# Layer 1's constants made, and its first aggregate loaded, inside layer 0; another order of steps and slots in layer 1

## The chip, the cores and the metric

The kernel runs on one core of one Trainium2 chip. The metric is the device time of one execution in microseconds (us). The engines are named as in the profile: PE (TensorE, with PEld for its weight loads), DVE (VectorE), ACT (ScalarE), POOL (GpSimd) and SP (SyncE, which issues most DMAs).

## What is computed

There are 16 graphs of 1024 nodes with 256 features each (`x`), and a sparse 0/1 adjacency matrix `adj` for each graph. Two layers follow one another, in fp32:

```python
# layer 0, for graph b
Wh  = x @ W.T;  att = (Wh @ a1)[:, :, None] + (Wh @ a2)[:, None, :]
att = bn(leaky(bn(att)));  att = softmax(att, axis=2) * adj
x   = layernorm(x + elu(bn(att @ Wh)))        # bn: statistics over all graphs
# layer 1, for each of 4 heads
fts    = x @ W[h];  logits = f1[:, :, None] + f2[:, None, :]
coefs  = al * softmax(leaky(logits) - 1e9 * (1 - adj)) + (1 - al) * softmax(adj)
out[h] = elu(coefs @ fts + bias[h] + x)
x      = layernorm(x + mean(out))
```

The last `bn` of layer 0 takes its statistics over all graphs and nodes, so layer 1 can't begin with any graph before the last graph of layer 0 is aggregated.

## The kernel before

**Layer 0** has three stages. From 0 to 185 us PE transposes x (`px`, L279) and multiplies it by the weights (`pw`, L289), eight tiles per graph in two halves. ACT copies the transposes (`xT`, L285) and DVE copies each product out of PSUM (`wx`, L293; four PSUM buffers). x comes by SP's queue with six buffers (`load_x`, L226), each load issued behind the store of an earlier graph's `wx` (L294). After graph 1, `parameters1` (L190ff) loads layer 1's small parameters by SP: `bias1`, `fb_bc` and `al_bc`. From 185 to 310 us thresholds and sums for the batch norms are made, and from 310 to 797 us the 16 graphs are aggregated one after another, 30 us each (L572). Each graph's aggregate `hb` is stored to `h_dram` (L599).

**Between the layers**, DVE finishes the statistics (scale `s3` and shifts `t3` and `t31`; last line L1023), and then makes layer 1's constants in the pool `pk` (L1036 to L1134): `IW`, `MX`, `MY`, `bits`, `add`, `cols`, `far`, `rows`, `low`, `act`, `lanes`, `fws`, `xr`. One of them needs a load: `wl`, the last row of each head's weights, broadcast over the partitions (512 KB, L1120), is subtracted from `W1s` (L1122). `wl` has a buffer of the tag `rw` (two buffers), which the rows of the adjacency matrix use too. The tag `h` in `hpool` has one buffer.

**Layer 1** is written under a manual schedule: on each engine, instructions stand in the order of the program. For each graph there are 16 units (8 node tiles times 2 pairs of heads), and the loop at the end of the kernel goes over slots, one unit per slot. Unit n starts in slot n - 1 and ends in slot n + 11. Its steps, in order of their work:

- `gather` (L1550, PE): multiplies the gathered rows `xc` by the weights `w` into `pu` (three PSUM buffers); `invert` (L1608, DVE) takes the reciprocal `z`, and `norm` (L1616, ACT) makes `s`, `pu` scaled by `z`, in two or three instructions.
- `turn` and `turned` (L1622 PE, L1632 ACT) transpose `s` into `sT`; `linear` (L1642, PE) multiplies it by `W1s` into `pv`; `add` (L1650, DVE), `exps` (L1656, ACT) and `sum` (L1663 to L1671, DVE) make the elu and the mean over the heads.
- `mean`, `squares`, `span`, `power`, `close` and `store` (L1678 to L1712; DVE, ACT, DVE, POOL, ACT, SP) make the last layer norm and store it.

Beside the units of graph g, the side work for graph g + 1 is done: it is placed by the tables `AT`, `FETCH` and `WEIGH`, whose numbers are slots relative to that graph's first unit (a number of -28 is slot 4 of the graph two before, modulo 16). `side` sorts it into four lists, `early`, `first`, `after` and `late`, which `stand(0..3, n)` emits:

- neighbour lists: `load_rows` (L1147, SP, 1 MB each) brings half of the adjacency rows `rw`; `words` (L1156, PE) packs them into words `pc`; `worded` (L1167 ACT `fw`, L1171 DVE `wl`) copies them out; then come `places` and `placed` (`hi`, L1200), `low`, `high`, `pick` and `picked` (`po`, L1259, PE), `order`.
- the graph's input of layer 1: `exps` and `elu` of the aggregate `h` (L1418 and L1421 ACT, L1428 DVE; four pieces), `turn` (`pz`, L1434, PE), `residual` (L1444, DVE, with x loaded at L1403), `squares` (L1461, ACT, four at a time), `spans`, `factors`, `raised` (L1500 to L1503, ACT), `scale` (L1481, ACT, eight instructions, four to each half), `halve` (`xs`, L1516, DVE), `total` and `totalled` (`pX`, L1524 PE; `xr`, L1527 ACT), and the stores of the table `xe_dram` (L1508, L1509, L1530).
- the neighbours: `fetch` (L1338, POOL) gathers rows of that table by indirect DMA, five times for each of eight chunks and a few times for the shared groups `l`, `m`, `n` and `o`; `weigh` (L1353 to L1382 DVE, with one cast on ACT, L1360) makes their weights.

An engine takes its instructions in order, so an instruction that waits holds up all that stand behind it on the same engine. `turned(n, f, then)` puts a PE step into `first[n]` and the step that reads its result into `early[n + 1]`.

Of the kernel before, what the change touches and what calls it, by code (L numbers as in the profile page):

```python
# [27 lines left out]
def kernel(  # L28
# [170 lines left out]

    with ExitStack() as l0:  # L200
# [17 lines left out]
        with tc.tile_pool(name="apool", bufs=1) as apool, tc.tile_pool(  # L218
# [86 lines left out]
            mts = {b: mask(mpool, b, "mt0") for b in range(min(2, B))}  # L305

# [210 lines left out]
        with tc.tile_pool(name="wk", bufs=1) as wk, tc.tile_pool(  # L517
# [89 lines left out]
            for b in range(B):  # L607
                for n in range(NH * K):
# [6 lines left out]
                    if n == 1 and b + 2 < B:  # L615
                        mts[b + 2] = mask(mpool, b + 2, "mt0")
                    if n == 1 and b > 0:
                        store(b - 1, NH - 1)
# [406 lines left out]
    with ExitStack() as l1:  # L1025
        xpool = l1.enter_context(tc.tile_pool(name="x1pool", bufs=3))
        hpool = l1.enter_context(tc.tile_pool(name="hpool", bufs=1))
# [5 lines left out]


        TW = P + 2 * H
        IW = pk.tile([P, C, TW], F32, name="IW")  # L1036
        for oc in range(C):
            nc.vector.tensor_copy(IW[:, oc, 0:P], ident)
        nc.vector.tensor_copy(IW[:, :, P:TW], WW)

        QR = (H + 1) * QB
        MX = pk.tile([P, H, QB], F32, name="MX")
        MY = pk.tile([P, H, QB], F32, name="MY")
        nc.vector.tensor_tensor(
            MX, ident[:, 0 : H * QB].rearrange("p (h q) -> p h q", h=H),
            al_bc.unsqueeze(2).to_broadcast([P, H, QB]), ALU.mult,
        )
        nc.vector.tensor_tensor(  # L1050
            MY, ident[:, H * QB : QR].unsqueeze(1).to_broadcast([P, H, QB]),
            om_bc.unsqueeze(2).to_broadcast([P, H, QB]), ALU.mult,
        )
        nc.vector.tensor_tensor(MX, MX, MY, ALU.add)

        bits = pk.tile([P, QB], F32, name="bits")
        for i in range(QB):
            nc.vector.memset(bits[:, i : i + 1], float(1 << i))  # L1060
        ibits = pk.tile([P, QB], I32, name="ibits")
        nc.vector.tensor_copy(ibits, bits)
        nc.vector.memset(bits[:, QB - 1 : QB], -float(1 << (QB - 1)))

        every = pk.tile([P, 1], I32, name="every")
        nc.vector.memset(every, (1 << QB) - 1)

        add = pk.tile([P, K, NB + 1], F32, name="add")
        pick = pk.tile([P, NB, QB], F32, name="pick")
        nc.vector.tensor_tensor(  # L1070
            pick, ident[:, 0 : NB * QB].rearrange("p (n q) -> p n q", n=NB),
            bits.unsqueeze(1).to_broadcast([P, NB, QB]), ALU.mult,
        )
        nc.vector.tensor_reduce(add[:, 0, 0:NB], pick, AX.X, ALU.add)
        nc.vector.tensor_copy(
            add[:, 1:K, 0:NB], add[:, 0, 0:NB].unsqueeze(1).to_broadcast([P, K - 1, NB])
        )
        last = pk.tile([P, K, 3], F32, name="last")
        nc.vector.tensor_tensor(
            last, ident[:, NB * QB : P].unsqueeze(1).to_broadcast([P, K, 3]),  # L1080
            bits[:, 0 : 3 * K].rearrange("p (k q) -> p k q", q=3), ALU.mult,
        )
        nc.vector.tensor_reduce(add[:, :, NB], last, AX.X, ALU.add)
        add16 = pk.tile([P, K, NB + 1], BF16, name="add16")
        nc.vector.tensor_copy(add16, add)


        cols = pk.tile([P, K, NQ], FP16, name="cols")
        jj = pk.tile([P, K, NQ], I32, tag="pi", name="jj", bufs=1)
        nc.gpsimd.iota(jj, pattern=[[P, K], [0, NQ]], base=-N, channel_multiplier=1)  # L1090
        nc.vector.tensor_copy(cols, jj)
        in8 = pk.tile([P, 8], F32, name="in8")
        nc.vector.tensor_reduce(in8, ident.rearrange("p (r q) -> p q r", q=8), AX.X, ALU.add)
        in8h = pk.tile([P, 8], FP16, name="in8h")
        nc.vector.tensor_copy(in8h, in8)
        in16 = pk.tile([P, 16], F32, name="in16")
        nc.vector.tensor_reduce(in16, ident.rearrange("p (r q) -> p r q", q=8), AX.X, ALU.add)
        in16h = pk.tile([P, 16], FP16, name="in16h")
        nc.vector.tensor_copy(in16h, in16)
        far = pk.tile([P, 24], FP16, name="far")  # L1100
        for i in range(24):
            nc.vector.memset(far[:, i : i + 1], float(2048 + P + 16 * i))


        rows = pk.tile([P, 9, 8], F32, name="rows")
        nc.vector.memset(rows, float(N))
        nc.vector.memset(rows[0:1, 0:NB, :], float(N + 1))
        nc.vector.memset(rows[0:1, 6, 0:1], float(N + 1))

        low = pk.tile([P, K, 48], FP16, name="low")  # L1110
        nc.vector.memset(low, 99.0)
        act = pk.tile([P, K + 1, NQ], BF16, name="act")
        nc.vector.memset(act, 0.0)
        lanes = pk.tile([P, 16, 8], FP16, name="lanes")
        for i in range(16):
            nc.vector.memset(lanes[:, i], float(i))


        wl = pk.tile([P, H, F], F32, tag="rw", name="wl", bufs=2)
# [7 lines left out]
        for i in range(2):  # L1127
            nc.vector.memset(fws[i][:, :, 0:1], 1.0)
# [758 lines left out]
```

The softmax here doesn't subtract the row's maximum and nothing guards it: scores larger than these inputs give would overflow.

## Time and profile before

| | |
|---|---|
| median of 3 runs | 2366.42 us (2366.23 to 2368.56) |
| profiled execution | 2364.92 us |
| its span | 2363.2 us |
| mean granted clock of PE | 0.917 |

| stage (us of the span) | length | PE busy | DVE busy | ACT busy | DMA share |
|---|---|---|---|---|---|
| 0 to 185: x·W | 185 | 157.78 | 69.62 | 36.04 | 0.85 |
| 185 to 310: sums and thresholds | 125 | 48.34 | 90.71 | 68.90 | 1.01 |
| 310 to 797: aggregate | 487 | 477.81 | 446.27 | 345.02 | 0.66 |
| 797 to 812 | 15 | 0.66 | 9.97 | 1.52 | 0.52 |
| 812 to 865 | 53 | 26.15 | 26.42 | 22.84 | 0.42 |
| 865 to 900 | 35 | 17.83 | 25.32 | 5.40 | 0.59 |
| 992.14 to 1084.28: one graph of layer 1 | 92.14 | 87.81 | 80.19 | 61.30 | 0.66 |

Lines of the profile read so: in a wait list, "A x L1 <- B y L2: total, times, longest" says that engine A stood idle before its instruction for x at line L1, until B's instruction for y at L2 was done. In a timeline, a line gives the start, the duration, the engine, the source line, the operation, what it writes and reads, and in brackets the idle time before it with what ended it. The busy time of PE includes matmuls that are modelled from their issue; a busy PE is not PE at its peak.

### The profile page before, as it was taken

The numbers are of one execution on the slowest core, as the hardware profiler recorded it, in microseconds if no ns is written. First come the engines' busy times: TensorE is split into PE (matmuls) and PEld (weight loads), VectorE is DVE, ScalarE is ACT, GpSimd is POOL, SyncE is SP. The second block draws the span as 40 slices with busy tenths as digits, with TensorE's granted clock in tenths as the row PEclk, the third lists the DMA queues.
The fourth block names the chain that finished last, engine by engine and source line by source line (L and its number), as shares of the span: only waits on it lengthen the run. The fifth ranks groups of instructions, "written<-read, shape, count | busy, mean of one in ns | idle before, by whom it ended". The sixth has DMA issues, their size and how long they took to land. (4 is left out here: it accounts for less than half of the span.)

```text
span 2363.2 us, 36997 instructions
## 1 busy us (share of the span) xinstructions
PE 2105.5 (89%) x12503; PEld 1647.8 (70%) x12503; DVE 1916.6 (81%) x4800; ACT 1435.5 (61%) x3028; POOL 1060.5 (45%) x1133
## 2 busy tenths in 40 slices
PE   6992479999999549899999999999999999999997
PEld 5772434444444338788888888788888788887886
DVE  3334899999999357888988989888889789898886
ACT  1122777777777226567676675675676666756665
POOL 0000100000000036776767766767767667667682
PEclk9995589999999758899999999999999999999999
DMA  8969959985553348576675685675666756756651
GB/s 258 285 191 236 263 115 244 226 206 154 155 155 93 116 147 215 160 179 174 171 196 177 157 213 162 161 206 160 181 176 172 198 162 163 210 166 164 138 149 52
DMA packets 342359, 419.75 MB, mean 178 GB/s; under 512 B 172760, under 2 KB 273168, under 8 KB 336016
## 3 DMA queue, kind: packets, MB, share of 16 engines
q1 hardware_dynamic: 285840, 256.24, 36.7%
q0 software_dynamic: 55104, 158.54, 30.4%
q10 hardware_dynamic: 1216, 2.51, 0.3%
q8 instruction: 101, 1.65, 0.3%
q14 instruction: 98, 0.80, 0.1%
HBM read 346.47 MB, written 104.29 MB: 191 GB/s over the span
## 5 line engine op out<-in xcount | busy, mean ns | idle before, releaser
L1338 POOL DMA_INDIRECT xc<-xe_dram,ix x640 | 690.7, 1079 | 184.8 <-issue 166.3
L1642 PE MATMUL pv<-W1s,sT 128*128 128x256 f32 x2048 | 504.6, 390 | 0.3 <-ACT sT L1636 0.3
L572 PE MATMUL pa<-em,wh 128*128 128x512 f32 x1024 | 451.3, 599 | 17.8 <-DVE em L536 13.4
L1642 PEld LDWEIGHTS pv<-W1s,sT 128*128 128x128 f32 x2048 | 381.6, 197 | 44.0 <-ACT sT L1636 0.7
L1622 PEld LDWEIGHTS pt<-MX,s 125*128 125x128 f32 x2560 | 355.3, 206 | 31.0 <-ACT sT L1632 9.1
L572 PEld LDWEIGHTS pa<-em,wh 128*128 128x128 f32 x1024 | 193.9, 192 | 250.4 <-issue 237.3
L1550 PE MATMUL pu<-xc,w 128*125 128x256 f32 x1280 | 365.4, 401 | 0.0
L1622 PE MATMUL pt<-MX,s 125*128 125x100 f32 x2560 | 355.6, 289 | 4.8 <-ACT sT L1632 2.9
L1656 ACT ACTIVATE m<-v,neg 128x512 f32<-128x512 f32 x256 | 184.1, 719 | 251.0 <-DVE v L1650 199.6
L1616 ACT ACTIVATE s<-pu,z 125x256 f32<-125x256 f32 x640 | 260.6, 472 | 113.3 <-DVE z L1608 63.3
L1550 PEld LDWEIGHTS pu<-xc,w 128*125 128x125 f32 x1280 | 238.6, 197 | 37.5 <-issue 6.1
L528 ACT ACTIVATE e<-eb,c,s 128x1024 f32<-128x1024 f32 x128 | 155.0, 1236 | 79.0 <-DVE sm L542 42.6
L1632 ACT COPY sT<-pt 128x500 f32<-128x500 f32 x256 | 147.1, 575 | 91.7 <-PE pt L1622 91.6
L1650 DVE TENSOR_TENSOR v<-pv,x 128x512 f32<-128x512 f32 x256 | 175.0, 683 | 8.2 <-PE pv L1642 7.9
L532 ACT ACTIVATE e<-e,v,u 128x1024 f32<-128x1024 f32 x128 | 152.3, 1229 | 22.7 <-DVE e L531 16.6
L1699 POOL TENSOR_TENSOR ors<-ors,mhalf 128x1 f32<-128x1 f32 x128 | 97.7, 764 | 149.2 <-DVE ors L1693 147.6
L536 DVE TENSOR_TENSOR em<-e,mt 128x1024 f32<-128x1024 f32 x128 | 155.6, 1218 | 3.4 <-PE pa L572 2.1
L1434 PE MATMUL pz<-IW,h 128*128 128x136 f32 x512 | 96.4, 324 | 68.1 <-DVE hi L1200 29.8
L531 DVE SCALAR_TENSOR_TENSOR e<-e 128x1024 f32<-128x1024 f32 x128 | 151.4, 1216 | 0.0
L1434 PEld LDWEIGHTS pz<-IW,h 128*128 128x128 f32 x512 | 81.7, 217 | 84.7 <-issue 46.2
L147 POOL TENSOR_TENSOR s<-var,mhalf 128x2 f32<-128x2 f32 x1 | 0.7, 710 | 311.9 <-DVE var L146 311.9
L293 DVE COPY wx<-pw 128x266 f32<-128x266 f32 x128 | 55.3, 434 | 98.3 <-PE pw L289 98.3
(320 smaller groups left out, 3558.8 us busy)
## 6 DMA issues: line engine op xcount, KB each, us to landing
x<-in_x_dram SPq DMA_DIRECT2D x32, 1024.0 KB
adj<-in_adj_dram POOLq DMA_DIRECT2D x16, 2048.0 KB
rw<-adj SPq DMA_DIRECT2D x32, 1024.0 KB
A<-u_dram SPq DMA_DIRECT2D x128, 250.0 KB
wh_dram<-wx SPq DMA_DIRECT2D x16, 1024.0 KB
wh<-wh_dram SPq DMA_DIRECT2D x16, 1024.0 KB
h_dram<-hb SPq DMA_DIRECT2D x16, 1024.0 KB
h<-h_dram SPq DMA_DIRECT2D x16, 1024.0 KB
```

The costliest lines, as they stand in the source:

```text
L528: nc.scalar.activation(e, ebs[b], AF.Identity, bias=c1[:, k, b : b + 1], scale=s1[:, k : k + 1])
L532: nc.scalar.activation(e, e, AF.Exp, bias=v2[:, k : k + 1], scale=u2[:, k : k + 1])
L536: nc.vector.tensor_tensor(em, e, mts[b][:, k, :], ALU.mult)
L572: nc.tensor.matmul(acc[b, hf, oc], wh[b][:, k, oc * P : (oc + 1) * P], ems[b, k][:, hf * HALF : (hf + 1) * HALF], start=(k == 0), stop=(k ...
L1338: nc.gpsimd.indirect_dma_start(out=self.xc[:, i, :], out_offset=None, in_=xe_dram[g.b % 2], in_offset=bass.IndirectOffsetOnAxis(ap=g.l.ix[ ...
L1434: nc.tensor.matmul(pz[:, oc, :], self.h[:, oc, k * P : (k + 1) * P], IW[:, oc, :], start=True, stop=True,)
L1550: nc.tensor.matmul(pu[0:QR, 0:F], c.w[:, k].rearrange("p h q -> p (h q)"), c.xc[:, k, 0:F], start=(i == 0), stop=(i == len(OF[q]) - 1),)
L1616: nc.scalar.mul(f.s[0:QR, i], f.pu[i][0:QR, 0:F], f.z[0:QR, i : i + 1])
L1622: nc.tensor.matmul(self.pt[:, i].rearrange("p h q -> p (h q)"), self.first.s[0:QR, i, self.hp * P : (self.hp + 1) * P], MX[0:QR].rearrange ...
L1642: nc.tensor.matmul(self.pv[:, hh, :], self.first.sT[:, fc, self.hp * HP + hh, :], W1s[:, fc, self.hp * HP + hh, :], start=(fc == 0), stop= ...
L1650: nc.vector.tensor_tensor(self.v2, self.pv, self.g.x[:, self.it].unsqueeze(1).to_broadcast([P, HP, F]), ALU.add)
L1656: nc.scalar.activation(self.m, self.v2, AF.Exp, bias=neg1, scale=1.0)
```

## The change

The instructions stay the same in number and kind; where they stand changes.

- Two pools, `ek` and `hpool`, are opened before layer 0 and closed after layer 1. The constants move from `pk` to `ek` and are written into layer 0's program text, after x·W. Layer 0's order is made by a scheduler: in the order that results, DVE makes the small constants between its copies of graphs 0 to 3, and the two subtractions of `wl` between those of graph 4. On SP, `wl`'s load stands behind x's tenth load, and the copy of a bias row into `W1s` behind the eleventh.
- `jj` and `wl` share the buffer of tag `h` with `h_0`; `wl` no longer takes one of the two `rw` buffers. `h_0`, graph 0's aggregate, is loaded right behind its store on SP, at about 364 us of the span before, and `load_h` of graph 0 only takes that tile.
- In layer 1, `words(0)` goes from -27 to -28, `rw` 1 from -28 to -29, the first `elu` from -26 to -28, the weighing of `o` from 0 to 1, and some fetches by one slot.
- The order of the steps in a slot is another.

```diff
+    m1 = ExitStack()
+    ek = m1.enter_context(tc.tile_pool(name="ek", bufs=1))
+    hpool = m1.enter_context(tc.tile_pool(name="hpool", bufs=1))
...
+        IW = ek.tile([P, C, TW], F32, name="IW")
...
+        jj = hpool.tile([P, K, NQ], I32, tag="h", name="jj")
...
+        wl = hpool.tile([P, H, F], F32, tag="h", name="wl")
+        nc.sync.dma_start(wl, W[:, F - 1, :].partition_broadcast(P))
+        for fc in range(C):
+            nc.vector.tensor_tensor(W1s[:, fc], W1s[:, fc], wl, ALU.subtract)
+        nc.sync.dma_start(W1s[P - 1 : P, C - 1], bias1[0:1])
...
+        h0 = hpool.tile([P, C, N], F32, tag="h", name="h_0")
...
+                    if n == 4 and b == B - 1:
+                        nc.sync.dma_start(h0, h_dram[0])
...
-        hpool = l1.enter_context(tc.tile_pool(name="hpool", bufs=1))
...
-        IW = pk.tile([P, C, TW], F32, name="IW")
...
-        wl = pk.tile([P, H, F], F32, tag="rw", name="wl", bufs=2)
...
             def load_h(self):
                 b = self.b
+                if b == 0:
+                    self.h = h0
+                    return
...
-            'lh': -29, ('rw', 0): -29, ('rw', 1): -28, ('words', 0): -27, ('words', 1):
+            'lh': -29, ('rw', 0): -29, ('rw', 1): -29, ('words', 0): -28, ('words', 1):
...
-            'mean': (-17, -14), 'elu': (-26, -25, -24, -23), 'turn': (-22, -21, -19,
+            'mean': (-17, -14), 'elu': (-28, -25, -24, -23), 'turn': (-22, -21, -19,
...
-            'l': (-7,), 0: (-7, -6, -6, -6, -6), 'm': (-6, -6, -5, -5, -4), 'n': (-4,
-            -4), 1: (-4, -3, -3, -3, -3), 'o': (-2, -2), 2: (-1, -1, 0, 0, 0), 3: (1, 1,
-            1, 1, 2), 4: (2, 3, 3, 3, 3), 5: (3, 4, 4, 4, 5), 6: (5, 5, 6, 6, 7), 7: (7,
+            'l': (-7,), 0: (-7, -6, -6, -6, -6), 'm': (-6, -6, -5, -4, -4), 'n': (-4,
+            -4), 1: (-3, -3, -3, -3, -3), 'o': (-2, -2), 2: (-1, 0, 0, 0, 0), 3: (0, 1,
+            1, 1, 2), 4: (3, 3, 3, 3, 3), 5: (4, 4, 4, 4, 5), 6: (5, 5, 6, 6, 7), 7: (7,
...
-            'l': -5, 0: -3, 'm': -2, 'n': -1, 1: 0, 'o': 0, 2: 2, 3: 4, 4: 6, 5: 8, 6:
+            'l': -5, 0: -3, 'm': -2, 'n': -1, 1: 0, 'o': 1, 2: 2, 3: 4, 4: 6, 5: 8, 6:
...
             for n in range(-EARLY, len(units) + 12):
+                do(n - 6, "add")
                 do(n - 9, "power")
-                do(n - 6, "add")
                 stand(0, n)
                 do(n - 6, "exps")
                 do(n - 3, "turn", "turned")
+                stand(2, n)
+                do(n - 7, "mean")
+                do(n - 8, "span")
+                do(n - 10, "close")
+                do(n - 5, "linear")
                 do(n - 1, "invert")
+                do(n - 11, "store")
                 do(n - 1, "norm")
-                stand(2, n)
-                do(n - 10, "close")
-                do(n - 11, "store")
-                do(n - 5, "linear")
                 if 0 <= n < len(units):
                     units[n].gather(0)
                 stand(1, n)
-                if 0 <= n < len(units):
-                    units[n].gather(1)
-                do(n - 7, "mean")
-                do(n - 8, "span")
                 stand(3, n)
                 do(n - 6, "sum")
                 do(n - 7, "squares")
+                if 0 <= n < len(units):
+                    units[n].gather(1)
+    m1.close()
```

## The prediction

> **What bounds the kernel now.** I read the page first, then the table of stages, then the wait list of layer 1's steady part, and last the timelines of four places that the change touches: the start of layer 0, the passage between the layers, and two slots of layer 1.
>
> The page's first block:
>
> ```profile
> span 2363.2 us, 36997 instructions
> ## 1 busy us (share of the span) xinstructions
> PE 2105.5 (89%) x12503; PEld 1647.8 (70%) x12503; DVE 1916.6 (81%) x4800; ACT 1435.5 (61%) x3028; POOL 1060.5 (45%) x1133
> ```
>
> TensorE (PE) is busy 89% of the span. By stages: 158 of the first 185 us (x·W), 48 of the next 125, 478 of 487 in the aggregate, 0.66 of 15 just after it (797 to 812 us), 26 of 53 after that, 18 of 35, and then about 87 of each graph's 92.14 us in layer 1 (the distance of the same instruction in successive graphs). So there are two places to gain: the passage between the layers, and some 5 us of idle PE per graph of layer 1. The wait list from 900 to 2340 us (total us, times, longest) says what those 5 us are:
>
> ```profile
> DVE wl L1171 <- ACT fw L1167: 56.1, 14, 4.1
> ...
> PE pz L1434 <- DVE hi L1200: 28.1, 14, 3.3
> ...
> PE pz L1434 <- DVE sl L1563: 22.9, 14, 1.9
> ```
>
> Once per graph DVE stands 4.1 us at `wl`, and PE stands about 2 us at each of two later turns. The wait at `wl` is not PE's, but it lies upstream of the two that are. The passage, in the timeline from 798 to 866 us:
>
> ```profile
> 802.25 10.48 SPq L1147 DMA_DIRECT2D rw<-adj  x2
> ...
> 811.34 0.99 PE L1156 MATMUL pc<-add,rw 128*128 128x6 bf16 x32 [15.11 <-DVE xr L1134]
> ...
> 818.28 1.01 PE L1156 MATMUL pc<-add,rw 128*128 128x6 bf16 x32 [5.95 <-DMA rw<-adj]
> ...
> 822.37 0.42 DVE L1444 CUSTOM_DVE_ANT_0 x<-pz,x 128x256 f32<-128x256 f32 x1 [2.52 <-DMA x<-in_x_dram]
> ```
>
> DVE makes constants until 811.2; its two subtractions of `wl` (issued 801.80) wait for that load and start at 808.52. `wl` holds one of the two "rw" buffers, so the second rw goes out only at about 812.7, and x after it, at 814.13; both 1 MB loads come late, and DVE's first residual waits for x until 822.37. From there DVE is nearly without a gap until 838.5.
>
> **The passage.** The 115 constant instructions (9.4 us), `wl` and its two subtractions leave. Both rw loads go out at 801.8, one after another, and x behind them. The next pair of rw, issued at 844.15 on quiet queues, let the words start at 849.70, so 5.5 us for the first. Hence rw_0 at 801.8 + 5.5 = 807.3, the second 1 MB 3.3 us later at about 300 GB/s (0.5 + 1 MB by about 810), x another 3.5 us later: 814. The first residual starts at 814.3 instead of 822.37: 8.1 us earlier. Its other input is ready: eight activations of exps on ACT (0.8 us each, 6.5 us) can start at 802, since `h_0` was already loaded before (issued at 768.9) and ACT stood only behind `fw`. So the early load of `h_0` is worth nothing by itself. SP now stands at that load until the store of h has landed (3.5 us by the one such wait in SP's own list) with the next `eb` load behind it at 365; the first use of that is a graph of 30 us away, cost 0; without that cover 3.5 us. Given back: the next graph's words and elu now stand ahead of `raised`, behind an rw load that comes 5.5 us after the order matmuls `po`; at the end of the passage (`xr`) I find 0.7 us of it. Gain 8.1 - 0.7 = 7.4 us, bounds 4.5 (the given-back part is the 2.9 us by which `raised` itself comes later, and x lands 0.7 us late) and 9.4.
>
> **Layer 0's first 185 us.** The small constants land between DVE's evictions of x·W, each followed by a gap: 0.43 us of copy, 0.46 us idle. 7 us of them spread over graphs 0 and 1, where gaps of 0.46 and 1.7 us occur eight times per graph: cost 0, or 1 us if a gap overflows, since four PSUM buffers (0.9 us each) lie between. `wl` is the exception. It is queued on SP behind x's tenth load, whose issue ends at 57.55 + 3.12 = 60.7 us, and DVE reaches the subtraction after the second eviction of graph 4, at 66.9 us. What a 512 KB broadcast takes here, the trace shows for `bias`:
>
> ```profile
> 42.63 1.62 SPq L191 DMA_DIRECT2D bias<-in_L_gnn_bias_dram  x1
> ...
> 54.17 0.69 DVE L192 TENSOR_SCALAR bias<-bias 128x1024 f32<-128x1024 f32 x1 [2.08 <-DMA bias<-in_L_gnn_bias_dram]
> ...
> 58.66 0.17 DVE L196 TENSOR_SCALAR om_bc<-al_bc 128x4 f32<-128x4 f32 x1 [3.71 <-DMA al_bc<-in_L_gnn_alpha_dram]
> ```
>
> 11.5 us from issue to use, and al_bc 11.9. PE waited 1.83 us for the eviction and started again at 59.35; less the 0.29 of its usual wait there it lost 1.5 us when evictions due at 54.0 came at 58.8, 4.8 us late. By that row `wl` lands at 60.7 + 11.5 = 72.2, the subtraction ends at 73.4, and the eviction due at 67.35 is 6.1 us late: 1.5 + 1.3 = 2.8 us of PE. MX and MY (0.43 us) now stand behind al_bc ahead of the late evictions: 0.3 us. PE sets the pace of this stage, so I let it through to the end: +3.1 us. By the passage's own `wl` (801.80 to 808.52, 6.7 us) it would land at 67.4, and the cost is 0.3; if it lands at 74, 4.5. I take the bias row, since the DMA share is above 1.0 from 48 to 72 us, as it was for bias.
>
> The Trainium skill, "DMA: Bandwidth & Descriptors", section "Anatomy of one DMA — SWDGE (gpsimd) path", fits one DMA (on the gpsimd path) at 2.0 us plus bytes over 436 GB/s; an estimate from it is 3.2 us for `wl`, before 66.9 even behind 1 MB of x, so no stall and a total 2.8 us lower; the bias row, 11.5 us for the same bytes, contradicts it here, and the row decides.
>
> **Layer 1, 14 steady graphs.** The instructions are the same ones and PE's order too, except that `words(0)` stands one slot earlier. On ACT, in the order before:
>
> ```profile
> 1198.00 4.04 ACT L1481 ACTIVATE x<-x,rs 128x256 f32<-128x256 f32 x8
> 1201.93 0.60 ACT L1706 ACTIVATE o<-o,ors 128x256 f32<-128x256 f32 x1
> 1202.42 0.29 ACT L1167 CAST fw<-pc 128x160 int32<-128x160 f32 x1
> ```
>
> `fw` stands behind eight scale steps, DVE stands at `wl` for it from 1198.6 to 1202.75 (4.12 us), and behind `wl` are queued the halvings, weigh, add and the next list. From there a chain runs: `xr` 1212.10, its store, the gather of `xc_l` 1217.44, the gathers behind it on POOL, last weights 1232.74, `hi` 1237.2, PE's turn 1237.84, `sl` 1240.16, PE's turn 1240.22. Now words, `fw` and elu stand a slot earlier, so DVE's 4.12 us at `wl` go; but the halvings next to it need the eight scales, whose start hangs on PE's slot, so most of the wait moves to them. I count what ACT no longer does between: one `fw` (0.29) and one activation of exps (0.8, which now comes earlier) ahead of `xr`: 1.1 us earlier, 0.9 to 1.3 by how `s` falls in between, and PE's two idle stretches (1.54 and 1.68) shrink by it. That the gathers' starts are 1.26 us apart and hang on `xc_l` speaks for passing it on.
>
> The loss: `norm` (the unit's `s`, three ACT instructions, 1.20) now stands behind `stand(2)`, which in slot 15 holds four squares (1254.15 to 1256.57, 2.4 us) and in slot 5 the scales. Behind `s` on ACT stand only this slot's weight casts and squares, but PE waits for `s` to free one of three `pu` buffers: its gather at 1255.85 would come at about 1256.8, less the 0.46 us that it already waits next for w_n: 0.5 to 0.95 us, take 0.6. In slot 6 the same costs 0.7 to 1.2 us, which I let vanish in the idle stretches downstream (slot 13). `mean` and `span` ahead of `z` on DVE are two instructions of 0.13: nothing. The later `xc_1` and `xc_2` fetches go by POOL's issue, with idle time of 0.3 us or more ahead: nothing, half a us if not.
>
> Net 1.1 - 0.6 = 0.5 us per graph, times 14 = 7 us. Bounds: a loss of 0.9 (0.9 gained, less 0.6, less the slot 6 delay of 1.2 in full) and a gain of 2.0 (the two idle stretches go, 3.2, less 0.6 and less as much again in slot 6); times 14, a loss of 13 and a gain of 28.
>
> **Sum** against the profiled run (2364.92 = span 2363.2 + 1.7): -7.4 + 3.1 - 7.0 = -11.3, so 2353.6; the median lies 1.5 us above the profiled run: 2355. A measurement of this kernel can tell about 0.2%, 4.7 us, from no change.
>
> **Rivals.**
> *Slower: ACT's order.* `s` behind `stand(2)` makes PE wait in slots 0 and 6 of every graph, 0.95 + 1.2 = 2.15 us, and nothing absorbs it; against the 1.1 gained that is 1.05 x 14 = +14.7, so 2364.9 - 7.4 + 3.1 + 14.7 + 1.5 = 2377. It decides from a net loss of (4.3 + 4.7) / 14 = 0.64 us per graph. For it: ACT `s` has 62.1 us of waits for `z` already, so it is late as it is. Against: PE has idle stretches later in each graph. 0.17.
> *Larger gain.* The 4.12 us at `wl` pass on in good part, and the matmuls after PE's idle stretches, slow now (pz 1.27 against 0.70), quicken as well: 2.3 us x 14 = 32, so 2330. For it: the chain above has no other long wait. Against: the scales. 0.22.
> *The passage alone.* The period stays 92.14, since something else closes the loop (POOL's gathers): 2364.9 - 7.4 + 3.1 + 1.5 = 2362. 0.16, of which 0.05 falls below 2361.7.
> My forecast, between 2340 and 2361: 0.45. Faster 0.45 + 0.22 + 0.05 = 0.72, same 0.11, slower 0.17. With every bound at one end the sums are 2364.9 - 9.4 + 0.3 - 28 + 1.5 = 2329 and 2364.9 - 4.5 + 4.5 + 13 + 1.5 = 2379. The range stops short of both and leaves out a part of the larger gain and of the slower case, about 0.1 each: 2334 to 2375.
>
> **What would show it.** PE's words in the passage at about 807.3 + the shift of layer 0, the first residual 8 us earlier; a DVE wait of 5 us for `wl` near 67 us and PE idle 3 us after it; no wait at `wl` in layer 1, but one at `xs`; a period of 91.6 us; `pz` waits of 0.5 to 1 us each; a new PE wait for ACT `s` at a `pu` gather. I am wrong if the period moves by over 2 us, if `s` costs PE over 1 us per graph, or if `wl` lands before 67 us.

## The result, and the profile after

The changed kernel takes 2389.73 us (median of 4 runs, 2388.62 to 2391.41) against 2367.49 us for the kernel before beside it: a ratio of 1.0085 [1.0069, 1.0102], so 22 us slower, where 12 us faster was predicted. The profiled execution took 2388.62 us with a span of 2386.9 us, at a mean granted clock of 0.922 (before 0.917), so the clock is not the reason.

The first block of its page:

```profile
span 2386.9 us, 36996 instructions
## 1 busy us (share of the span) xinstructions
PE 2103.8 (88%) x12503; PEld 1638.9 (69%) x12503; DVE 1920.8 (80%) x4800; ACT 1437.1 (60%) x3028; POOL 1043.5 (44%) x1133
```

PE, DVE and ACT are as busy as before to within 4.2 us, with as many instructions, and the span is 23.7 us longer: the loss is waiting. Its place is read from the starts of the order matmuls `po` (one group per graph) in PE's timeline:

| stretch | before | after | difference |
|---|---|---|---|
| start to the end of layer 0's last shift `t31` | 801.8 | 806.3 | +4.5 |
| from there to the first `po` | 36.4 | 28.7 | -7.7 |
| first to second `po` | 62.5 | 66.0 | +3.5 |
| second to last `po`, 14 graphs | 1300.2 | 1325.5 | +25.3 |
| last `po` to the end | 162.3 | 160.4 | -1.9 |

So the passage gained what was expected of it, and layer 0 and the first graph lost all of it again (-7.7 + 4.5 + 3.5); the 14 steady graphs went from 92.87 to 94.68 us each, and that is the whole result. (The prediction's 92.14 was the distance of one pair of graphs; the mean of before is 92.87.) Single periods run from 91.7 to 94.6 us before, and from 92.4 to 97.7 after.

The passage, in the timeline after:

```profile
806.29 0.95 SPq L1155 DMA_DIRECT2D rw<-adj  x2
...
812.20 0.99 PE L1164 MATMUL pc<-add,rw 128*128 128x6 bf16 x32 [11.47 <-DMA rw<-adj]
...
814.71 1.02 PE L1164 MATMUL pc<-add,rw 128*128 128x6 bf16 x32 [1.52 <-DMA rw<-adj]
...
818.92 0.41 DVE L1455 CUSTOM_DVE_ANT_0 x<-pz,x 128x256 f32<-128x256 f32 x1
...
867.51 0.42 DVE L1455 CUSTOM_DVE_ANT_0 x<-pz,x 128x256 f32<-128x256 f32 x1 [6.35 <-DMA x<-in_x_dram]
```

Both `rw` loads go out together at 806.29, PE's words start 5.9 us later (predicted 5.5), and the first residual stands 12.6 us behind the end of layer 0 instead of 20.6, with no wait for x. But the next graph's first residual waits 6.35 us for its x.

The start of layer 0 after, DVE's and PE's lines in order of time:

```profile
55.49 0.17 DVE L196 TENSOR_SCALAR om_bc<-al_bc 128x4 f32<-128x4 f32 x1 [4.02 <-DMA al_bc<-in_L_gnn_alpha_dram]
...
72.00 1.23 DVE L400 TENSOR_TENSOR W1s<-W1s,wl 128x1024 f32<-128x1024 f32 x1 [7.97 <-DMA wl<-in_L_gnn_W_dram]
...
73.72 3.60 PE L294 MATMUL pw<-WX,xT 128*128 128x266 f32 x8 [5.13 <-DVE wx L298]
```

DVE stands 7.97 us at the first subtraction of `wl`, and PE waits 5.13 us for the copy queued behind it.

The wait list from 900 to 2340 us:

```profile
POOL ors L1710 <- DVE z L1619: 189.7, 35, 7.4
...
ACT s L1627 <- DVE z L1619: 96.2, 68, 5.8
DVE x L1455 <- DMA x<-in_x_dram: 53.7, 12, 6.7
...
PE pz L1445 <- DVE fs L1462: 23.0, 14, 2.4
...
PE pz L1445 <- DVE ors L1704: 22.7, 14, 1.7
...
DVE wl L1179 <- ACT fw L1175: 19.9, 21, 2.6
...
PE pu L1561 <- ACT s L1627: 19.4, 27, 2.0
PE pp L1191 <- DVE act L1183: 18.2, 11, 2.2
...
DVE xs L1527 <- ACT x L1492: 13.0, 17, 1.4
PE pz L1445 <- DVE hi L1208: 12.3, 10, 2.9
```

The wait at `wl` fell from 56.1 to 19.9 us, as meant. But PE's waits at its turns (`pz`) are not less: 23.0 + 22.7 + 12.3 = 58.0 us against 28.1 + 22.9 + 5.6 = 56.6. A wait that was of little weight before has grown: the residual for x, 53.7 us in 12 graphs, and behind it PE's wait for `act`, DVE's next step for the neighbour lists. Before, the rows read:

```profile
DVE x L1444 <- DMA x<-in_x_dram: 11.0, 7, 3.8
...
PE pz L1434 <- DVE fs L1451: 5.6, 6, 2.2
...
PE pp L1183 <- DVE act L1175: 5.4, 4, 2.3
```

One such place after, SP's issue of x and DVE's wait for it in the timeline:

```profile
1501.69 1.59 SPq L1414 DMA_DIRECT2D x<-in_x_dram  x1
...
1519.12 0.42 DVE L1455 CUSTOM_DVE_ANT_0 x<-pz,x 128x256 f32<-128x256 f32 x1 [6.73 <-DMA x<-in_x_dram]
```

x takes 17 us from issue to use here. Over the steady graphs it lands 11.3 us after its issue before and 15.6 us after. The issue stands 0.9 us earlier in the graph (34.4 us after `po` against 35.3), so the load got slower, not later.

### The profile page after: what moved, and what is told of

Its sections match the earlier page's. It is cut to its first block, busy times and chain, and to the rows that moved or that the text cites. A ratio compares the mean times of both kernels' runs of the same rounds, so it can differ in the third digit from the quotient of the medians.

```text
span 2386.9 us, 36996 instructions
## 1 busy us (share of the span) xinstructions
PE 2103.8 (88%) x12503; PEld 1638.9 (69%) x12503; DVE 1920.8 (80%) x4800; ACT 1437.1 (60%) x3028; POOL 1043.5 (44%) x1133
## 5 line engine op out<-in xcount | busy, mean ns | idle before, releaser
L1346 POOL DMA_INDIRECT xc<-xe_dram,ix x640 | 679.1, 1061 | 185.2 <-issue 156.3
L1561 PE MATMUL pu<-xc,w 128*125 128x256 f32 x1280 | 367.1, 400 | 19.5 <-ACT s L1627 19.4
L1633 PE MATMUL pt<-MX,s 125*128 125x100 f32 x2560 | 349.1, 287 | 2.4 <-ACT sT L1643 2.4
L1561 PEld LDWEIGHTS pu<-xc,w 128*125 128x125 f32 x1280 | 232.0, 194 | 64.8 <-ACT s L1627 30.8
L643 ACT ACTIVATE e<-e,v,u 128x1024 f32<-128x1024 f32 x128 | 152.3, 1229 | 22.7 <-DVE e L642 16.6
L1445 PEld LDWEIGHTS pz<-IW,h 128*128 128x128 f32 x512 | 77.9, 207 | 89.1 <-issue 47.2
L294 PE MATMUL pw<-WX,xT 128*128 128x266 f32 x512 | 125.9, 399 | 14.5 <-ACT xT L290 9.4
```

The lines of the kernel that those rows point to most:

```text
L643: nc.scalar.activation(e, e, AF.Exp, bias=v2[:, k : k + 1], scale=u2[:, k : k + 1])
L1346: nc.gpsimd.indirect_dma_start(out=self.xc[:, i, :], out_offset=None, in_=xe_dram[g.b % 2], in_offset=bass.IndirectOffsetOnAxis(ap=g.l.ix[ ...
L1445: nc.tensor.matmul(pz[:, oc, :], self.h[:, oc, k * P : (k + 1) * P], IW[:, oc, :], start=True, stop=True,)
L1561: nc.tensor.matmul(pu[0:QR, 0:F], c.w[:, k].rearrange("p h q -> p (h q)"), c.xc[:, k, 0:F], start=(i == 0), stop=(i == len(OF[q]) - 1),)
L1633: nc.tensor.matmul(self.pt[:, i].rearrange("p h q -> p (h q)"), self.first.s[0:QR, i, self.hp * P : (self.hp + 1) * P], MX[0:QR].rearrange ...
```

## The experiments

Four theories were weighed; the expectations name them by letters. **N** is the prediction's slower rival: the new order of steps puts `norm` behind `stand(2)`, and PE waits for `s`. **X**: x lands late, and DVE waits for it. **F**: the new fetch slots move gathers out of a quiet stretch into the one where the 1 MB loads run. **W**: `words`, `fw`, the list steps and the first elu now stand ahead of the chain factors, `raised`, scale, table, and the table comes later. The expectations of the f, g and h runs call W by the letter A (not the chip); the first one also has **M**, the move itself, and the last two part W into W (words and `fw`) and **E** (the elu).

The runs were made on chips that differ. On chip A the kernel before takes 2352.47 us. On chips B, C and D it takes 2540.39, 2539.67 (with the second set on C 2540.05) and 2540.93 us: there layer 1 is slower for every kernel (102.4 us a graph with the old tables and steps, 92.1 on A) while layer 0 is not. "Period" below is the mean distance of `po` over 13 graphs, from the second on, in the profiled execution. All ratios are against the kernel before on the same chip, and sizes are not carried from A to the others.

### Which part of the change costs the time (chip A)

Layer 0's move alone, with the old tables and the old order of steps:

```diff
+    ek = m1.enter_context(tc.tile_pool(name="ek", bufs=1))
...
+        wl = hpool.tile([P, H, F], F32, tag="h", name="wl")
...
+                        nc.sync.dma_start(h0, h_dram[0])
...
-        wl = pk.tile([P, H, F], F32, tag="rw", name="wl", bufs=2)
```

> The changed kernel with layer 1's tables and step order as they were before; only the constants, wl and h_0 are made in layer 0. Three theories for the slower kernel. X: in layer 1 the load of x takes 15.6 us from issue to landing instead of 11.3, because POOL's gathers now run beside it without a pause, and DVE's first residual waits for it; each us of lateness lengthens the graph's period by about one. N (a rival of the prediction): ACT's norm behind stand(2) makes PE wait for s, 0.6 + 0.77 us per graph, and that is the loss. M: the move into layer 0 itself slows layer 1. X and N expect the period of before, 92.9 us, and a time of before + 4.5 (stage x.W) - 7.7 (passage) + 0 to 3.5 (given back in the first graphs), 2363 to 2368 us. M expects the period of 94.7 us and about 2390 us.

Measured: 2352.62 us, 0.9998 [0.9986, 1.0011]; period 92.07. The move itself does not slow layer 1: M falls.

The whole change, but with the steps of a slot in the old order (cut to one of its moves):

```diff
                 do(n - 3, "turn", "turned")
-                stand(2, n)
...
                 do(n - 1, "norm")
+                stand(2, n)
```

> The changed kernel with the order of steps within a slot as before, but the new tables AT, FETCH and WEIGH. N expects PE's waits for s to go and with them the loss: a period near 92.9 us and 2363 to 2370 us. X goes by the tables if they are what moves the gathers: POOL then still has one fetch per graph behind its wait for ors, x still lands 15 us or more after its issue, the residual still waits 2 us or more for x in most graphs, and the time stays at 2380 to 2390 us. If X holds but the steps are what moves the gathers, x lands after 11 to 12 us and the time is 2363 to 2370 us as in N, and the waits for x tell the two apart.

Measured: 2371.80 us, 1.0083 [1.0058, 1.0107]; period 93.55. This is the whole loss of the changed kernel without its new order.

The whole change, but with the old tables `AT`, `FETCH` and `WEIGH`:

```diff
-            'lh': -29, ('rw', 0): -29, ('rw', 1): -29, ('words', 0): -28, ('words', 1):
+            'lh': -29, ('rw', 0): -29, ('rw', 1): -28, ('words', 0): -27, ('words', 1):
...
-            'mean': (-17, -14), 'elu': (-28, -25, -24, -23), 'turn': (-22, -21, -19,
+            'mean': (-17, -14), 'elu': (-26, -25, -24, -23), 'turn': (-22, -21, -19,
...
-            -4), 1: (-3, -3, -3, -3, -3), 'o': (-2, -2), 2: (-1, 0, 0, 0, 0), 3: (0, 1,
+            -4), 1: (-4, -3, -3, -3, -3), 'o': (-2, -2), 2: (-1, -1, 0, 0, 0), 3: (1, 1,
```

> The changed kernel with the tables AT, FETCH and WEIGH as before, but the new order of steps within a slot. N expects the loss to stay, 2385 to 2392 us, with PE's waits for s of about 1.4 us per graph. X, where the tables move the gathers, expects x to land about 11.5 us after its issue, hardly a wait of the residual for it, and a period of 92.5 to 93.5 us, 2363 to 2372 us, although PE's waits for s remain.

Measured: 2352.79 us, 0.9999 [0.9986, 1.0012]; period 92.05. From its wait list:

```profile
DVE wl L1179 <- ACT fw L1175: 57.2, 15, 4.2
...
PE pt L1633 <- ACT s L1627: 15.6, 14, 1.1
...
PE pu L1561 <- ACT s L1627: 10.1, 14, 0.8
```

The new order does make PE wait for `s`: (15.6 + 10.1) / 14 = 1.8 us per graph. Yet the time is unchanged. **N falls** on this chip: its wait is real and lies on no path that sets the end. In the second of the three kernels, where the wait list has this instead,

```profile
POOL xc_l L1346 <- DMA xe_dram<-xr: 35.8, 10, 5.4
...
DVE x L1455 <- DMA x<-in_x_dram: 18.4, 10, 4.3
DVE wl L1179 <- ACT fw L1175: 18.2, 14, 2.3
```

the wait at `wl` is gone as predicted (57.5 us in the kernel with the move alone), PE's `pu` waits for `s` are only 1.1 us, and the loss is there. So it lies in the three tables.

What the new `AT` does is read from ACT's timeline at the same place of a graph, first with the old tables (the move alone, `po` at 1265.52), then with the new ones (old order, `po` at 1270.94):

```profile
1285.38 4.04 ACT L1492 ACTIVATE x<-x,rs 128x256 f32<-128x256 f32 x8
...
1289.80 0.29 ACT L1175 CAST fw<-pc 128x160 int32<-128x160 f32 x1
```

```profile
1289.07 0.28 ACT L1175 CAST fw<-pc 128x160 int32<-128x160 f32 x1
...
1292.76 4.03 ACT L1492 ACTIVATE x<-x,rs 128x256 f32<-128x256 f32 x8
```

`fw` stands ahead of the eight scales now, and the scales themselves start 21.8 us after `po` instead of 19.9 in this graph, where they are the latest of all 14. As means over the steady graphs, the scales start 20.9 us after `po` against 19.5, `raised` 20.5 against 19.2, the store of the table's `fw` part 26.4 against 25.1, and that part has landed at about 37.1 against 35.4. DVE's wait was not spent on the way to the table before; now a shorter one is. Most of this delay is gone by the first gather, `xc_l`: 38.5 us after `po` against 38.1.

### Is x's lateness the cause?

x loaded three slots earlier in the changed kernel:

```diff
-            ... 'order': -11, 'lx': -23, 'spans': -12,
+            ... 'order': -11, 'lx': -26, 'spans': -12,
```

> The changed kernel with the load of x three slots earlier (lx at -26 instead of -23), where the trace shows SP without DMAs and the DMA engines half busy; nothing else differs. X expects the wait of the residual for x to vanish in layer 1, every period at 92.5 us or below (as the graphs have it now in which that wait is shortest), and 2350 to 2360 us. N and M expect 2385 to 2392 us, since s and the move are as they were.

Measured: 2394.09 us, 1.0180 [1.0157, 1.0203]; period 95.07, slower still. x now lands 7.5 us after its issue and no residual waits for it, but two rows have grown that were 5.6 and 2.9 us in the changed kernel:

```profile
POOL xc_l L1346 <- DMA xe_dram<-fw: 62.4, 12, 7.9
DVE mi L1361 <- DMA xc<-xe_dram,ix: 56.0, 13, 5.6
```

x is in flight from 20.6 to 28.1 us after `po`, where the table is stored, and the table's `fw` part lands at about 41 us instead of 36; the first gather of the next graph waits for that. X's forecast, 2350 to 2360 us, **fails**: an earlier load is no cure. That does not clear the late x in the changed kernel itself. Positions in the graph, as means over the same 13 graphs (us after `po`), show where the delay enters:

| | before | changed | move alone (A) | old order (A) | old tables (A) | x earlier (A) |
|---|---|---|---|---|---|---|
| first gather, `xc_l` | 38.8 | 37.5 | 38.1 | 38.5 | 37.3 | 41.6 |
| x has landed | 46.6 | 50.1 | 45.7 | 48.4 | 45.7 | 28.1 |
| first residual | 47.2 | 50.2 | 46.7 | 48.5 | 46.3 | 46.1 |
| `hi` | 59.4 | 60.8 | 58.7 | 60.0 | 58.3 | 61.4 |
| next `po` | 92.87 | 94.67 | 92.07 | 93.55 | 92.05 | 95.07 |

From `hi` to the next `po` it is 33.3 to 33.9 us in all six, so the loss is made ahead of `hi`. DVE reaches `hi` behind the residual, which needs x, and behind the weighing, which needs the gathers. In the changed kernel the gathers come earlier than before and x later; with x loaded earlier it is the other way round. In both kernels that lose by the tables the residual is late with x (3.0 us, and 1.8 with the old order). Graph by graph it is the same: in the changed kernel the two shortest graphs (92.4 us) have their first residual 47.8 and 48.3 us after `po`, the two longest (97.7 and 97.1) at 53.1 and 53.0.

### The tables one by one (chips B, C and D)

> The changed kernel itself, beside the other three on their chip. All theories expect 1.007 to 1.010 on a chip like the first, and a loss as large as or larger than the 1.038 of the kernel without x where layer 1 is slow as in the runs at 2540 us.

The changed kernel itself on chip C: 2616.74 us, 1.0305 [1.0244, 1.0367]; period 107.8. The loss is three and a half times as large here.

New `AT` and new order with the old `FETCH` and `WEIGH`, run on B and again on C:

```diff
...
-            -4), 1: (-3, -3, -3, -3, -3), 'o': (-2, -2), 2: (-1, 0, 0, 0, 0), 3: (0, 1,
+            -4), 1: (-4, -3, -3, -3, -3), 'o': (-2, -2), 2: (-1, -1, 0, 0, 0), 3: (1, 1,
...
```

> The changed kernel with FETCH and WEIGH as before; AT (words, rw and elu a slot or two earlier) and the step order stay new. The tables as a whole made the loss (1.008 with them, 1.000 without). Theory F: the later fetches of chunks 4 and 5 move two gathers per graph from the 8 us about the order matmuls, where the DMA engines are half idle, to the 20 us behind them, where the table, x and A are moved and the engines are full. F expects the loss to go: a ratio of 0.998 to 1.002 to the kernel before, and x landing within about 11 us. Theory A: words and elu ahead of raised put the scales, the table and everything behind it later. A expects the loss to stay, 1.006 to 1.010.

> The changed kernel with FETCH and WEIGH as before, AT and the step order new, again: in its first run all kernels, the one before too, were some 8% slower in layer 1 (2540 us against 2352 and 2367), with ACT standing up to 7 us before copies whose input was ready, so that its ratio, 1.013, can't be set beside the others. F (the later fetches move gathers out of the half idle 8 us about the order matmuls into the full 20 us behind them) expects 0.998 to 1.002; A (words and elu ahead of raised) expects 1.006 to 1.010.

Measured: 1.0131 [1.0056, 1.0205] and 1.0099 [1.0070, 1.0127]; the table's store goes out about 31 us after `po`, against 26 with the old tables on C. The old fetch slots take most of the loss away here; F had expected them to take all of it.

The other half, the old `AT` with the new fetch slots and the new order (B):

```diff
-            'lh': -29, ('rw', 0): -29, ('rw', 1): -29, ('words', 0): -28, ('words', 1):
+            'lh': -29, ('rw', 0): -29, ('rw', 1): -28, ('words', 0): -27, ('words', 1):
...
```

> The changed kernel with AT as before; FETCH, WEIGH and the step order stay new. F expects the loss to stay, 1.006 to 1.010, with no gathers in the 8 us about the order matmuls and x landing 14 us or more after its issue. A expects the loss to go, 0.998 to 1.002.

Measured: 1.0391 [1.0315, 1.0468], which neither theory expected; period 110.55, the longest of all, with the table's store at 25 us, as early as before. In the first 8 us after `po` POOL issues no gather here; the kernel with the old fetch slots issues 3 there (4 in the trace of before, and 1 in that of the changed kernel). On chip A this count is no mark of the loss: it is 4 in the move alone, and 3 both with the old tables, which lose nothing, and with the old order, which loses all.

The loss of 3 to 4% on these chips also enters at another place than that of the result. From `hi` to the next `po` it is 39.3 to 40.0 us in all kernels with the new fetch slots and the new order here (this run, the changed kernel, and the next two pairs), and 33.6 to 34.0 in all others on B, C and D. The excess lies in one stretch, from the last turns to the seventh residual of a graph, 10.7 us in the changed kernel on C against 6.2 with the old tables and steps there and 5.9 in the result's own trace; in it ACT stands 5.2 us per graph at its copies `sT`. So these runs do not tell which table costs the 0.85% of the result.

Only the first fetches of chunks 4 and 5 put back into their old slots (B, C):

```diff
-            1, 1, 2), 4: (3, 3, 3, 3, 3), 5: (4, 4, 4, 4, 5), 6: (5, 5, 6, 6, 7), 7: (7,
+            1, 1, 2), 4: (2, 3, 3, 3, 3), 5: (3, 4, 4, 4, 5), 6: (5, 5, 6, 6, 7), 7: (7,
```

> The changed kernel with only the first fetches of chunks 4 and 5 back in their earlier slots (2 and 3 instead of 3 and 4). F expects most of the loss to go, 1.000 to 1.003; A, and a form of F in which the other fetches (m, 1, 2, 3) matter, expect 1.006 to 1.010.

> The changed kernel with only the first fetches of chunks 4 and 5 back in slots 2 and 3, again for the same reason (1.032 there). F in its narrow form, two gathers per graph, expects 1.000 to 1.003; if the other moved fetches matter as much, 1.004 to 1.007; A expects 1.008 to 1.010.

Measured: 1.0316 [1.0258, 1.0373] and 1.0306 [1.0271, 1.0341], the changed kernel's own 1.0305. These two fetches are not it on these chips.

No loads of x for graphs 3 to 15, 13 MB in all:

```diff
             def load_x(self):
+                if b > 2:
+                    self.x = graphs[b - 3].x
+                    return
```

> The changed kernel without the loads of x in layer 1 for graphs 3 to 15 (1 MB each; the residual works on the tile of an earlier graph, so its values differ). If the late x, by its wait and by its share of the full DMA engines, is what costs the time, the wait of the residual goes and the time falls to 0.995 to 1.002 of the kernel before. If x is only a sign of it and the loss comes by the table (xe_dram) and the chain behind it, the time falls by less than 8 us, to 1.004 or above.

> The changed kernel without the loads of x in layer 1 for graphs 3 to 15 (the residual works on the tile of an earlier graph, so its values differ), again for the same reason (1.040 there). If the late x itself is the cost, and not only a sign of full DMA engines, 0.995 to 1.002. If the wait merely moves on to the gathers and the table, as it did when x was loaded three slots earlier (1.018, with the table landing 7 us later), 1.004 or above.

Measured: 1.0395 [1.0340, 1.0450] and 1.0384 [1.0348, 1.0420]. It is no faster than the changed kernel with its loads (1.0305), so x's load is not the bound on these chips; there x lands 9.0 us after its issue in the changed kernel, and no residual waits for it.

Then each table alone on the kernel before, without the move and without the new order. `FETCH` and `WEIGH`:

```diff
-            -4), 1: (-4, -3, -3, -3, -3), 'o': (-2, -2), 2: (-1, -1, 0, 0, 0), 3: (1, 1,
+            -4), 1: (-3, -3, -3, -3, -3), 'o': (-2, -2), 2: (-1, 0, 0, 0, 0), 3: (0, 1,
...
-            'l': -5, 0: -3, 'm': -2, 'n': -1, 1: 0, 'o': 0, 2: 2, 3: 4, 4: 6, 5: 8, 6:
+            'l': -5, 0: -3, 'm': -2, 'n': -1, 1: 0, 'o': 1, 2: 2, 3: 4, 4: 6, 5: 8, 6:
```

> The kernel before with the new FETCH and WEIGH alone. F expects most of the loss: 1.005 to 1.009 of the kernel before, fewer gathers in the 8 us after the start of the order matmuls (4 before) and x landing 48 us or later after that start (45 to 47 before). A expects 0.998 to 1.002.

Measured: 0.9984 [0.9964, 1.0004], no loss; 3 gathers in the first 8 us. **On these chips the fetch slots cost only together with the new order of steps**: the run with the old `AT` had added that and the move, and the move alone, in a form with `wl` loaded first, costs nothing (next section). The new order with all the old tables was not run here, so that the order alone costs on these chips is not excluded; with the new `AT` it adds nothing (1.0099 with it, 1.0095 below without).

`AT` alone, that is both of its edits:

```diff
-            'lh': -29, ('rw', 0): -29, ('rw', 1): -28, ('words', 0): -27, ('words', 1):
+            'lh': -29, ('rw', 0): -29, ('rw', 1): -29, ('words', 0): -28, ('words', 1):
...
-            'mean': (-17, -14), 'elu': (-26, -25, -24, -23), 'turn': (-22, -21, -19,
+            'mean': (-17, -14), 'elu': (-28, -25, -24, -23), 'turn': (-22, -21, -19,
```

> The kernel before with the new AT alone (words and first elu earlier, second rw in the slot of the first). A expects most of the loss: 1.005 to 1.009, with the stores of the table issued 1 us or more later after the order matmuls. F expects 0.998 to 1.002.

Measured: 1.0095 [1.0061, 1.0128]; period 104.36, the table's store at 31 to 33 us. So `AT` costs by itself here. How it does so is not what the result's trace shows: on these chips ACT starts `fw` a median of 4.6 us after the recorded end of the words' matmuls and stands idle for 4.3 us of that (0.2 us, and nothing, in the changed kernel of the result), and with `fw` ahead of `raised` that idle time makes the table late. Its two halves (chip D): the first of the two edits, the words a slot earlier,

> The kernel before with words(0) at -28 and the second rw at -29 alone. Theory W (DVE's wait at wl now stands ahead of the factors, so raised, the scales and the table come later) expects 1.004 to 1.010 and the table's store at least 1 us later after the order matmuls. Theory E (the exps and elu ahead of raised do it) expects 0.998 to 1.003.

measured 1.0011 [0.9988, 1.0034], though the table's store goes out at 31.5 us (in a profiled execution that was the slowest of the 12); and the second, the first elu two slots earlier,

> The kernel before with the first elu at -28 alone. E expects 1.004 to 1.010 (two activations of 0.8 us on ACT and one instruction of 0.7 us on DVE now stand ahead of raised); W expects 0.998 to 1.003. If both come out at 1.003 to 1.006, the two share the loss.

measured 2526.08 us, 0.9934 [0.9909, 0.9960]: **faster than before**, with the table at 26 us. Neither half costs what W and E expected (1.004 to 1.010), and the parts do not add up: +0.1% and -0.7% alone, +0.95% together. W's mark, the late table, appears with the words alone; its price does not.

### What layer 0's stalls cost, and a version that is faster (chip C)

The move alone, with `wl` loaded ahead of the first load of x, and old tables and steps (chip C):

```diff
+            wl = hpool.tile([P, H, F], F32, tag="h", name="wl")
+            nc.sync.dma_start(wl, W[:, F - 1, :].partition_broadcast(P))
```

> The changed kernel with the tables and step order of before, and wl loaded ahead of all loads of x (jj has a tile of its own). In the changed kernel wl landed at 71.97 us, 11.4 us after its issue, and PE stood 5.13 us for the eviction behind it; with the old tables and steps the move alone came out at 1.000. With wl first the stall near 67 us should go and, if it reaches the end, the time falls by 4 to 5 us to 0.997 to 0.999; at most 1 us is lost at the start, as x lands later. If the first graphs of layer 1 take it back as they take back the passage's 7.7 us, it stays at 1.000.

Measured: 2543.15 us, 0.9998 [0.9963, 1.0033]. From DVE's timeline:

```profile
29.60 1.22 DVE L400 TENSOR_TENSOR W1s<-W1s,wl 128x1024 f32<-128x1024 f32 x1
...
55.63 0.69 DVE L192 TENSOR_SCALAR bias<-bias 128x1024 f32<-128x1024 f32 x1 [6.05 <-DMA bias<-in_L_gnn_bias_dram]
...
61.20 0.17 DVE L196 TENSOR_SCALAR om_bc<-al_bc 128x4 f32<-128x4 f32 x1 [4.54 <-DMA al_bc<-in_L_gnn_alpha_dram]
```

The stall at `wl` is gone, and DVE waits 6.05 us for `bias` and 4.54 us for `al_bc` instead; the stall only moved to the next loads in SP's queue. So all four small loads went ahead, behind the third load of x:

```diff
+                if b == 2:
+                    nc.sync.dma_start(wl, W[:, F - 1, :].partition_broadcast(P))
+                    parameters1()
...
-                if b == 1:
-                    parameters1()
...
-        wl = hpool.tile([P, H, F], F32, tag="h", name="wl")
-        nc.sync.dma_start(wl, W[:, F - 1, :].partition_broadcast(P))
```

> The move into layer 0 alone (tables and steps of before), with wl and the small parameters (bias, fb_bc, al_bc) loaded behind the third x. In the move alone PE stood 4.4 us for evictions behind wl; with wl first it stood 2.0 and 4.2 us behind bias and al_bc, whose loads then took 15 to 17 us. With all of them early no DVE instruction of x.W should wait for a load, the stage should end some 4 us earlier than in the move alone, and the time fall to 0.997 to 0.999. If the first graphs of layer 1 take it back, 1.000.

Measured: 2528.16 us, 0.9943 [0.9916, 0.9970], **faster than before**. DVE's timeline has no wait at any of them:

```profile
28.44 0.69 DVE L192 TENSOR_SCALAR bias<-bias 128x1024 f32<-128x1024 f32 x1
...
30.21 0.16 DVE L196 TENSOR_SCALAR om_bc<-al_bc 128x4 f32<-128x4 f32 x1
...
34.40 1.21 DVE L400 TENSOR_TENSOR W1s<-W1s,wl 128x1024 f32<-128x1024 f32 x1
```

Against the run with `wl` first, the first `po` starts at 829.5 instead of 836.2 and the second at 911.4 instead of 919.8. That is 8 of the 15 us between the medians of these two runs; the profiled executions lie only 3.3 us apart, so where the rest falls is not settled.

## Why the prediction was wrong, point by point

- **Layer 1, the step that failed.** The sum had a gain of half a microsecond per graph; the period grew by 1.8 us, 25.3 over 14 graphs, twice the 13 that the text gave as its bound for a loss. The first links of its chain (`wl`, `xr`, gather of `xc_l`, last weights, `hi`, PE's turns) held: the wait at `wl` fell from 56.1 to 19.9 us, `xr` is stored 1.1 us earlier (32.7 against 33.7 us after `po`; 1.1 predicted), the first gather starts 1.3 us earlier, and the waits of POOL's `xc_l` for `xr`, 45.5 us before, are down to 1.1. What failed is the next link: the text let the last weights, and so the gathers, decide when `hi` comes. In the changed kernel DVE stands for x at the first residual, ahead of `act` and `hi`, 3.0 us later than before, and `hi` comes 1.4 us later although the gathers come earlier. The load of x is no term of the sum for these graphs. The term that touched it was put too low: moved fetches cost "nothing, half a us if not", priced on POOL's issue alone, while each gather is also a load on the DMA engines, and that was left out of the price. On chip A the three tables carry the whole loss, and the new order of steps none. A second step, the words, `fw` and the elu put ahead of factors, `raised` and the scales at no price in the steady graphs, shows on A with the old order (store of the table 1.3 us later, first gather 0.4 us), but not in the changed kernel's own trace, where the store (25 us after `po`) and its landing (36 us) are where they were.
- **Where those gathers went.** As means over the steady graphs, POOL's DMAs held the DMA engines at a share of 0.40 from 4 to 8 us after `po` before and 0.04 after. From 40 to 44 us, with x under way, it was 0.21 before and 0.45 after, and the share of SP's DMAs, x among them, went from 0.81 to 0.55. That x then takes 4.3 us longer to land is measured; that the gathers' DMA time does it, and not the order of some queue, is supported by these shares and by the earlier x, which delayed the table by 5 us, but was not shown for each gather. With the old order on chip A POOL's share from 40 to 44 us is 0.25, against 0.22 in the move alone, and x still lands 2.7 us later in the graph: what makes it late there is open.
- **The rival "ACT's order" had the sign and the wrong mechanism.** Its wait for `s` came (19.4 us in 27 waits, 1.4 us per graph, over the 1 us that the text named as a sign of being wrong). On chip A it costs nothing with the old tables, and the loss is the same without it.
- **The passage.** The first residual comes 8.0 us earlier after the end of layer 0 (8.1 predicted), and the first `po` 7.7. The term that was mis-sized is the given-back part: 0.7 us was put down for the words ahead of `raised`, and 3.5 us went at the next graph, whose x landed at 867.38 us, as late as before (867.84). With the old tables (the move alone, chip A) the first `po` comes 2.5 us later than in the changed kernel (837.5 against 835.0) and the second 2.0 us earlier (899.0 against 901.0): the earlier slots bought a part of the first gain and gave back more.
- **Layer 0.** `wl` landed at 71.97 us (predicted 72.2) and held DVE up as described. PE lost 5.13 - 0.29 = 4.8 us, not 2.8: the sum counted on an eviction 6.1 us late, and DVE stood 7.97 us at `wl`. The first aggregate matmul of layer 0 came at 303.49 instead of 298.84, so the loss went through to the end, as the text had it: +4.5 against +3.1.
- **The rule weighed there.** The Trainium skill's fit for one DMA ("DMA: Bandwidth & Descriptors", "Anatomy of one DMA — SWDGE (gpsimd) path") is made on the gpsimd path and gave an estimate of 3.2 us for `wl`; the trace of after shows 11.43 us on SP's queue, and the measurement decides.
- **The move alone.** By the prediction's own terms it was worth -7.4 + 3.1 = -4.3 us; the interval of its ratio, 0.9986 to 1.0011, is -3.3 to +2.6 us. With the terms of the changed kernel's trace, -7.7 + 4.5 = -3.2 us is at the edge of that. The part of the change with the best reason behind it brought no gain that could be measured; its own loads took most of it back.

What stays open: how the 0.85% divides between `AT` and `FETCH` on chip A, where they were not parted, and so what makes x late there; which fetch costs under the new order on the other chips; why the words and the elu cost together what neither does alone; and whether the two faster versions gain on chip A, where they were not run.

## What to carry to other kernels

A wait is not a loss to be removed: ask first whether what will stand in its place is queued ahead of work that the next graph's transfers need. Price every moved DMA twice, by its issue on the queue and by the stretch of the DMA engines that it leaves and enters; in a stretch with full engines some other load can come late, as x and the table did here, and the wait then shows under that load's name. When an in-order engine needs two inputs before a step, gathers and x here, ask which comes last after the change and not only before it. A load moved into an early stage here had to be put ahead of the large loads of its queue, together with its neighbours, or the stall only changed its name.

## What was not expected of the hardware

The same 512 KB broadcast took 6.7 us from issue to use on a quiet queue (`wl` before), 11.43 us behind loads of x on full engines, and `bias` took 15.0 us in the run with `wl` first; there the 2 KB of `al_bc` took 17 us. In these cases the price of a small load went with what was ahead of it and not with its size; its queue and the full engines were not parted.

On chips B, C and D layer 1 was some 11% slower for every kernel, with the clock at 0.90 instead of 0.92 and layer 0 unchanged. In the traces there, ACT reads the result of the words matmuls late (the move with `wl` first, timeline):

```profile
1277.30 0.94 PE L1164 MATMUL pc<-add,rw 128*128 128x6 bf16 x32
...
1285.49 0.30 ACT L1175 CAST fw<-pc 128x160 int32<-128x160 f32 x1 [6.54 <-remote]
```

ACT had been idle for 6.54 us, and the matmuls' recorded end lies at 1278.24; the median lag there is 5.9 us, against 0.1 us in the changed kernel of the result and in the two runs with the new tables on A. What makes it was not found. It means that a schedule's price is one chip's: the same change cost 0.85% on one and 3% on another.
